# A graph-attention layer on one core: 128 dense groups instead of 120, counted by halves, with the counting moved ahead of the third and fourth tile's scores

## The chip, the core and the metric

The kernel runs on one core of a Trainium2 chip. The engines are named as in the profile: PE (matrix multiply; PEld is its weight load), DVE (vector), ACT (scalar), POOL (here the issuer of the indirect gathers) and SP (issuer of the other DMAs). The metric is the device time of one execution in microseconds, lower is better.

## The reference

The layer has 12,500 nodes of 64 features and 400,000 directed edges, each with 64 features of its own. The edges are sorted by destination, and destinations are drawn unevenly: the first nodes have hundreds of edges each, the last ones few.

```python
h_src = nfeats[src]; h_dst = nfeats[dst]
e = leaky_relu(concat([h_src, h_dst, efeats]) @ W_attn + b_attn, 0.01)[:, 0]
m = concat([h_src, efeats]) @ W_ne
ex = exp(e - segment_max(e, dst)[dst])
alpha = ex / segment_sum(ex, dst)[dst]
z = segment_sum(alpha[:, None] * m, dst)
out = relu(concat([nfeats, z]) @ W_out)
result = layernorm(nfeats + out)
```

What costs time is `nfeats[src]`, a gather of 400,000 rows, together with a softmax and a sum over each destination's edges.

## The kernel before

**Groups, parts, tiles.** The sorted edges are cut into 782 groups of 512 (128 partitions by T = 4). The first 120 groups (`DG`) are "dense": so few destinations fall in each that they are handled without a gather. The other 662 are "main" groups. These are worked in 43 parts: 39 of 16 groups, then 10, 10, 12 and 6 (`ENDS`). A part of 16 has four tiles of four groups, so 16 gathers for each tile and 64 for the part. One gather is one indirect DMA of 128 rows (L337), issued by POOL in program order. A part's gathers have the "places" 0 to 63.

**One part.** The loop over parts does, for tile i = 0 to 3: `scores` (L374 to L401; it multiplies edge features with a weight row, reduces them, adds the gathered source term at L390, and picks the destination's term by a one-hot row, L392 to L400), and between tiles work of other groups. Then comes one `softmax` of the part (L711 to L800; the maximum and the sum over destinations are scans over a row of 128 numbers, taken to a line and back by PE, L615 and L618). It is a generator: at four of its steps `drawn` calls `dense_step(n)`, n = 0 to 3, so that other work stands in the engines' queues between the softmax's own instructions. Then `weights` makes the one-hot times alpha (L808), and `products` (L820, L825) and `add_in` (L844) of each tile are laid into the next part's window and softmax. "Window" here means the stretch from the first L808 of a part to the next part's softmax; it is where the four tiles' scores are.

**What holds the gathers back.** POOL would run as far ahead as the buffers allow. `STEPS` and `PROBES` hold it: `step(place)` notes the matmul that stands last in PE's queue at that point, and the gather of that place then waits for it. The noted points are, with their places: the softmax's step 0 (8), the products in it (11, 14, 19, 24), the lookups (16, 21, 51), the counts (28, 33, 54), products (37 to 46) and the edge sums (48, or 57 with node products). A probe lets gather place+4 wait until PE has read what gather `place` brought (L328). Parts 1 and up are noted; the notes are cleared at part 1.

**Dense groups.** They go through four stages, several parts apart, in rounds of 12 (`ROUNDS`).
- *Look* (four groups a part, then three): `look_turn` on ACT makes a one-hot of the source's low seven bits, `look_products` (L460) multiplies it with the source terms of all blocks of 128 nodes, `look_scores` (L485 to L491) picks the block on DVE; `look_rows` (L470 to L479) adds the edge term. It gives each dense edge its score.
- *Joined*: a finished round's scores ride along in one part's softmax.
- *Count* (`dense_counts`): for each of the four t, ACT makes a one-hot over (block, node in group) in two passes (L499, L500), DVE a one-hot of the low bits times alpha (`lows`, L502), and PE multiplies the two (L507). The result, 98 columns for each node of the group, up to five nodes together and the sixth and seventh apart (L512 to L515), is added into `counts` by `dense_sum` (L525, L528).
- *Edges and nodes*: `edge_products`/`edge_sum` (L568, L577) sum the edge features. When a chunk of groups is counted, `node_products` (L584, 50 matmul instructions) multiplies `counts` with all node features, and `node_pick`, `node_turn`, `node_sum` (L592 to L609, with a clearing of `counts`, L597) take it to the accumulator.

**Order.** Nothing is reordered: each engine runs its instructions as the program writes them, and waits for operands and for buffers (four PSUM banks under the name `pg`, six `big` and six `lows` tiles).

## Time and profile before

| | |
|---|---|
| median of 3 runs | 4025.86 us (4024.07 to 4028.93) |
| the profiled execution | 4021.27 us, of which the span of instructions is 4019.5 us |
| granted PE clock, mean | 0.663 |
| PE / PEld / DVE busy | 60% / 50% / 53% |
| ACT / POOL busy | 32% / 62% |
| gathers L337 | 2584 on the page and 64 of part 0 before the table is made |

No engine is busy for more than 62% of the span. So the shares alone don't say what sets the time; it has to be read from who waits for whom within one part. A part's softmax begins with its ACT instruction L713, so the distance between two of them is the time of one part. In the rows, "128x490" is partitions by elements, "[2.78 <-PE lines L618]" is idle time before an instruction and what ended it, and "issue" means that nothing the profile shows was waited for.

### The profile page before, as it was taken

The numbers are of one execution on the slowest core, as the hardware profiler recorded it, in microseconds if no ns is written. First come the engines' busy times: TensorE is split into PE (matmuls) and PEld (weight loads), VectorE is DVE, ScalarE is ACT, GpSimd is POOL, SyncE is SP. The second block draws the span as 40 slices with busy tenths as digits, with TensorE's granted clock in tenths as the row PEclk, the third lists the DMA queues.
The fourth block names the chain that finished last, engine by engine and source line by source line (L and its number), as shares of the span: only waits on it lengthen the run. The fifth ranks groups of instructions, "written<-read, shape, count | busy, mean of one in ns | idle before, by whom it ended". The sixth has DMA issues, their size and how long they took to land. (4 is left out here: it accounts for less than half of the span.)

```text
span 4019.5 us, 39047 instructions
## 1 busy us (share of the span) xinstructions
PE 2404.4 (60%) x10302; PEld 1993.8 (50%) x10302; DVE 2133.3 (53%) x5517; ACT 1291.2 (32%) x2835; POOL 2511.9 (62%) x2676
## 2 busy tenths in 40 slices
PE   0144355665656676676777676656766657576544
PEld 0133345555555565554556554545655545465443
DVE  5343444555555555555655555645656464554345
ACT  1111122332333333333333433233443333333212
POOL 7466666666666666666666666666666666666452
PEclk9999996555555566665666666656666666666655
DMA  9222232332333233332332222322333232222121
GB/s 115 61 62 58 57 65 61 63 64 63 68 65 76 59 76 63 72 69 64 65 66 62 61 62 61 70 61 61 69 69 68 55 66 52 53 53 52 35 47 28
DMA packets 515063, 250.70 MB, mean 62 GB/s; under 512 B 351226, under 2 KB 472409, under 8 KB 514834
## 3 DMA queue, kind: packets, MB, share of 16 engines
q1 hardware_dynamic: 426588, 159.37, 17.1%
q0 software_dynamic: 84960, 88.33, 13.3%
q8 instruction: 87, 1.43, 0.1%
q14 instruction: 142, 1.16, 0.1%
q10 hardware_dynamic: 3286, 0.40, 0.1%
HBM read 241.09 MB, written 6.79 MB: 62 GB/s over the span
## 5 line engine op out<-in xcount | busy, mean ns | idle before, releaser
L337 POOL DMA_INDIRECT zx<-table,srcs x2584 | 2441.3, 945 | 1423.8 <-issue 778.1
L825 PE MATMUL pg<-w,zx 128*128 128x16 f32 (+9 forms) x5152 | 1107.0, 387 | 130.8 <-issue 87.7
L825 PEld LDWEIGHTS pg<-w,zx 128*128 128x128 f32 x5152 | 1091.0, 323 | 152.1 <-issue 93.1
L507 PE MATMUL pg<-big,lows 128*128 128x490 f32 (+3 forms) x960 | 546.8, 738 | 358.8 <-issue 107.5
L507 PEld LDWEIGHTS pg<-big,lows 128*128 128x128 f32 x960 | 267.1, 293 | 583.8 <-issue 499.1
L499 ACT ACTIVATE big<-places,place 128x490 f32<-128x490 int16 (+3 forms) x480 | 293.9, 612 | 96.9 <-PE pg L460 55.0
L487 DVE TENSOR_TENSOR pr<-pr,pg 128x392 f32<-128x392 f32 x120 | 67.5, 562 | 472.0 <-remote 172.5
L460 PE MATMUL pg<-s_src,big 128*128 128x98 f32 x960 | 266.6, 444 | 51.8 <-issue 51.5
L328 PE MATMUL pps<-zx,ident 1*1 1x1 f32 x236 | 21.3, 159 | 422.8 <-DMA zx<-table,srcs 368.4
L460 PEld LDWEIGHTS pg<-s_src,big 128*128 128x128 f32 x960 | 240.0, 328 | 49.0 <-issue 48.1
L500 ACT ACTIVATE big<-big 128x490 f32<-128x490 f32 (+3 forms) x480 | 257.1, 536 | 15.3
L385 DVE TENSOR_REDUCE fixed<-pr 128x16 f32<-128x1024 f32 (+3 forms) x172 | 204.2, 1187 | 102.1 <-ACT fixed L380 29.5
L615 PE MATMUL lines<-ident,bnd 128*1 128x128 f32 x172 | 51.8, 404 | 344.9 <-issue 249.5
L328 PEld LDWEIGHTS pps<-zx,ident 1*1 1x1 f32 x236 | 9.5, 76 | 447.9 <-DMA zx<-table,srcs 361.8
L844 DVE TENSOR_TENSOR acc<-acc,pg 128x16 f32 (+9 forms) x662 | 122.9, 186 | 174.1 <-remote 82.5
L390 DVE TENSOR_TENSOR fixed<-fixed,zx 128x16 f32<-128x16 f32 (+3 forms) x172 | 31.7, 184 | 329.6 <-DMA zx<-table,srcs 304.3
L383 DVE TENSOR_TENSOR pr<-ze,lines 128x1024 f32<-128x1024 f32 (+3 forms) x172 | 201.2, 1170 | 3.6 <-DMA ze<-in_edge_dram 3.5
L380 ACT ACTIVATE fixed<-wrow 128x96 f32<-128x96 f32 (+11 forms) x172 | 45.1, 262 | 477.7 <-issue 172.9
L615 PEld LDWEIGHTS lines<-ident,bnd 128*1 128x1 f32 x172 | 11.6, 93 | 352.8 <-issue 263.7
L502 DVE TENSOR_SCALAR lows<-fixed,low,kept 128x128 f32<-128x128 f32 x480 | 164.0, 401 | 34.5 <-PE pg L507 17.3
L381 ACT ACTIVATE zx<-ze 128x1024 f32<-128x1024 f32 (+3 forms) x172 | 176.5, 1026 | 6.2 <-issue 0.7
L713 ACT ACTIVATE soft<-turned 128x128 f32<-128x128 f32 x43 | 16.7, 388 | 482.2 <-DVE sdst L400 159.2
(305 smaller groups left out, 3035.3 us busy)
## 6 DMA issues: line engine op xcount, KB each, us to landing
ze<-in_edge_dram SPq DMA_DIRECT2D x157, 512.0 KB
zx<-table,srcs POOLq DMA_INDIRECT x2584
low_of<-low_rows SPq DMA_DIRECT2D x120, 128.0 KB
ep<-in_edge_dram SPq DMA_DIRECT2D x120, 128.0 KB
ed<-in_edge_dram SPq DMA_DIRECT2D x21, 512.0 KB
ed<-in_edge_dram SPq DMA_DIRECT2D x12, 384.0 KB
table<-xall SPq DMA_DIRECT2D x7, 455.0 KB
out_dram<-yo SPq DMA_DIRECT2D x24, 128.0 KB
```

Source lines behind the costliest of these rows:

```text
L337: issued.append(nc.gpsimd.indirect_dma_start(out=zx[0:r, g, t, 1:EW] if plain else zx[0:r, g, t, 0:EW], out_offset=None, in_=x[:, :] if pl ...
L381: nc.scalar.activation(zx[0:r, 0:n, :, EW:EW + D], ze[0:r, 0:n], AF.Copy)
L383: nc.vector.tensor_tensor(pr[0:r, 0:n], ze[0:r, 0:n], w_edge[0:r].unsqueeze(1).to_broadcast([r, n, T, D]), op=OP.mult)
L385: nc.vector.tensor_reduce(ysum[0:r, 0:n], pr[0:r, 0:n], axis=AX.X, op=OP.add)
L460: at_hand[0] = nc.tensor.matmul(found[:, t, :], hot[:, :, t], s_src, start=True, stop=True).ins
L487: nc.vector.tensor_tensor(hits, hits, found, op=OP.mult)
L499: nc.scalar.activation(hi, places[:, 0:wide], AF.Square, bias=place[:, t, g:g + 1])
L500: nc.scalar.activation(hi, hi, AF.Relu, scale=-1.0, bias=1.0)
L502: nc.vector.tensor_scalar(lows[t], count_, low[:, t, g:g + 1], kept[:, t, kept_at(g):kept_at(g) + 1], op0=OP.is_equal, op1=OP.mult)
L507: at_hand[0] = nc.tensor.matmul(to, lows[t], highs[t], start=(t == 0), stop=(t == T - 1)).ins
L825: at_hand[0] = nc.tensor.matmul(pg[:, g, :], zx[:, g, t, 1:EW + D], w[:, g, t, :], start=(t == 0), stop=(t == T - 1)).ins
L844: nc.vector.tensor_tensor(ag, ag, pg[:, g, :], op=OP.add)
```

## The change

1. **Sizes.** 128 dense groups instead of 120, in 16 rounds (twelve of 8, then 9, 9, 9, 5); main groups fall from 662 to 654, in 42 parts: 40 of 16 groups, then 8 and 6. Lookups are four a part up to group 96, then three. There are 18 chunks of node products instead of 12. A part's softmax carries a round on every second part.
2. **Counts by halves.** The 512 edges of a group are seen as two halves (t = 0, 1 and t = 2, 3), each with a first node of its own (`firsts`, `t0i`) and 2, 3 or 4 nodes wide (`HALVES`). Each half has a PSUM bank; `dense_sum` adds two results, at two places of `counts`. The sixth and seventh nodes' extra columns are gone.
3. **Order.** The edge sum, the node pick, the first lookup's scores and the node turn move from the softmax's step 0 to the stretch ahead of tile 2's scores; the second count's rows are made there too, the third's right after those scores, and only a fourth count stays in softmax step 3. `look_rows` moves from tile 2 to tile 1. One `dense_sum` stands ahead of tile 2's scores and one ahead of tile 3's.
4. **Holds.** The places 28, 33 and 54 (counts) no longer hold a gather; parts 0 and 1 leave no notes and no probes.
5. **Lookups in 16 bits.** The one-hot is bf16 and the source terms are three bf16 parts that add up in PSUM: twelve matmuls of 16-bit data for a lookup in place of four in fp32.
6. **Others.** The dense list is turned by PE transposes instead of loaded by ten DMAs; dense edges are loaded as (t p), in pieces of one row, not of four; a round that rides along goes through two more PE transposes; block 0's finish starts as soon as it can.

The core of the diff:

```diff
-ROUNDS = (12, 12, 12, 12, 12, 12, 12, 12, 12, 12)
+ROUNDS = (8,) * 12 + (9, 9, 9, 5)
-EACHS = ((84, 4), (120, 3))
+EACHS = ((96, 4), (128, 3))
-CHUNKS = ((36, 1), (12, 2), (8, 3), (6, 6))
+CHUNKS = ((36, 1), (12, 2), (8, 3), (4, 3), (6, 2), (3, 6), (2, 1))
+HALVES = ((40, 2), (84, 3), (128, 4))
+J = 2
-STEPS = {"ends": 8, "tile0": (11, 14, 19, 24), "look0": 16, "look1": 21, "count2": 28, "count3": 33,
-         "now": (37, 40, 43, 46), "edges": 48, "look": 51, "count": 54}
+STEPS = {"ends": 8, "tile0": (11, 14, 19, 24), "look0": 16, "look1": 21,
+         "now": (37, 40, 43, 46), "edges": 48, "look": 51}
-    ENDS = ((3, 3, 2, 2), (3, 3, 2, 2), (3, 3, 3, 3), (2, 2, 1, 1))
+    ENDS = ((2, 2, 2, 2), (2, 2, 1, 1))
...
-        hot = big()
+        hot = work.tile([P, P, T], BF16, name="turn", bufs=2)
...
         for t in range(T):
-            at_hand[0] = nc.tensor.matmul(found[:, t, :], hot[:, :, t], s_src, start=True, stop=True).ins
+            for i in range(3):
+                at_hand[0] = nc.tensor.matmul(found[:, t, :], hot[:, :, t], s_parts[:, i], start=(i == 0), stop=(i == 2)).ins
...
+        tos = [spare()[:, 0:wide] for _ in range(J)]
         for t in range(T):
-            at_hand[0] = nc.tensor.matmul(to, lows[t], highs[t], start=(t == 0), stop=(t == T - 1)).ins
+            at_hand[0] = nc.tensor.matmul(tos[t * J // T], lows[t], highs[t], start=(t * J % T == 0),
+                                          stop=(t * J % T == T - J)).ins
...
-                in_full[0] = G == BS
-                if k == 1 or G < BS:
+                in_full[0] = G == BS and k > 1
+                if k == 2 or G < BS:
                     marks.clear()
...
                 for i, (g0, n) in enumerate(lots[k]):
+                    if i == 2:
+                        if summed:
+                            edge_sum(*summed)
+                            summed = None
+                        picked_ = node_pick(*opened) if opened else None
+                        if seen:
+                            look_scores(*seen.pop(0))
+                        if len(batch_counts) > 1:
+                            open_counts.append(dense_counts(batch_counts[1]))
+                        if opened:
+                            node_z = node_turn(*picked_)
+                            opened = None
...
+                    if i > 1 and open_counts:
+                        dense_sum(*open_counts.pop(0))
...
                     hot = scores(g0, n, tiles[i], drel, b0, k == 0)
+                    if i == 2 and len(batch_counts) > 2:
+                        open_counts.append(dense_counts(batch_counts[2]))
...
-                    if n == 0 and opened:
-                        opened = node_pick(*opened)
-                    if n == 0 and summed:
-                        edge_sum(*summed)
-                        summed = None
                     if seen:
                         look_scores(*seen.pop(0))
-                    if n in (0, 3):
+                    if n == 0:
                         while open_counts:
                             dense_sum(*open_counts.pop(0))
...
-                    if n > 1:
-                        for g in batch_counts[-2:-1] if n == 2 and len(batch_counts) > 2 else batch_counts[1:][-1:] if n == 3 else ():
-                            open_counts.append(dense_counts(g))
-                            step(STEPS[f"count{n}"])
+                    if n == 3 and len(batch_counts) > 3:
+                        open_counts.append(dense_counts(batch_counts[3]))
```

What this does to the engines' queues shows at two places. The first is DVE in a part with node products and an edge sum. Before, the head of the softmax's step 0, right behind the scans L715 and L716 and ahead of the scans L723 and L724, reads (the last rows of an edge sum, `look_scores`, and the first of two counts' sums; the node pick stands ahead of them):

```order
L577 ISA
L577 TENSOR_TENSOR acce<-acce,pg 64x4
L485 TENSOR_TENSOR pr<-fixed,high 128x392
L487 TENSOR_TENSOR pr<-pr,pg 128x392
L489 TENSOR_REDUCE picked<-pr 128x4
L491 TENSOR_TENSOR y_dense<-y_dense,picked 128x4
L520 TENSOR_LOAD rel
L525 ISA
L525 TENSOR_TENSOR counts<-counts,pg 128x98x5
```

Of the changed kernel, the same work in another such part, now between tile 1's and tile 2's scores (`L503` to `L509` is `look_scores`, `L521` the second count's `lows`, `L613` the clearing of `counts`, `L538` the sum of a half):

```order
L587 TENSOR_TENSOR acce<-acce,pg 64x4
L602 TENSOR_TENSOR pr<-pg,own 128x256
L605 TENSOR_REDUCE sums__10318<-pr 128x64
L503 TENSOR_TENSOR pr<-fixed,high 128x392
L505 TENSOR_TENSOR pr<-pr,pg 128x392
L507 TENSOR_REDUCE picked<-pr 128x4
L509 TENSOR_TENSOR y_dense<-y_dense,picked 128x4
L521 TENSOR_SCALAR lows<-fixed,low,kept 128x128 x4
L613 MEMSET counts 128x3136
L533 TENSOR_LOAD rel
L538 ISA
L538 TENSOR_TENSOR counts<-counts,pg 128x98x3
```

Behind these rows the second half's sum follows, and then tile 2's scores. Edge sum, pick, lookup and one count's sum have left the softmax for the window, and the lows of a second count, which used to be made in the window or in softmax step 2, now stand ahead of tile 2's scores in all parts with two or more counts.

The second place is PE in such a part's window and the softmax behind it. Before, the edge products, a lookup and two counts are followed by the probe, and then by the softmax with the node turn and the next lookup:

```order
L568 MATMUL pg<-wd,ep 128x10 x8
L460 MATMUL pg<-s_src,big 128x98 x4
L507 MATMUL pg<-big,lows 128x490 x8
L328 MATMUL pps<-zx,ident 1x1 x2
L615 MATMUL lines<-ident,bnd 1x4x32 x2
L820 MATMUL pg<-zx,ident 1x4x8
L825 MATMUL pg<-w,zx 128x32 x16
L603 MATMUL pg<-node,sums__14404 64x32
L460 MATMUL pg<-s_src,big 128x98 x4
L618 MATMUL lines<-ident,line 128x1 x2
```

Of the changed kernel, from the end of the first lookup:

```order
L478 LDWEIGHTS turn
L478 MATMUL pg<-s_parts,turn 128x98
L526 MATMUL pg<-big,lows 128x294 x8
L611 MATMUL pps<-node,sums__15088 64x32
L526 MATMUL pg<-big,lows 128x294 x4
L345 MATMUL pps<-zx,ident 1x1 x2
L625 MATMUL lines<-ident,bnd 1x4x32 x2
L835 MATMUL pg<-zx,ident 1x4x8
L840 MATMUL pg<-w,zx 128x32 x16
```

The first two counts and the node turn (`L611`) come ahead of the third count's four matmuls, all of them ahead of the probe `L345`, and the counts are 294 columns wide here instead of 490. Softmax step 0 has no node turn any more. The lookup's four fp32 matmuls have become pairs of a 16-bit weight load and a matmul.

More of the change, by code (lines that the diff above doesn't have):

```diff
@@ L880, in sorted_path @@
     lists[1] = listed(1)
-    ids = pre.tile([DG, P, 2 * T], I32, name="ids", bufs=1)
-    nc.sync.dma_start(out=ids, in_=idx[0:DG])
+    ids = [pre.tile([min(P, DG - a), P, 2 * T], I32, name=f"ids{a}", bufs=1) for a in range(0, DG, P)]
+    for a, part in zip(range(0, DG, P), ids):
+        nc.sync.dma_start(out=part, in_=idx[a:min(a + P, DG)])
+    t0i = pre.tile([1, DG * J], I32, name="t0i", bufs=1)
+    nc.sync.dma_start(out=t0i, in_=dst.rearrange("(o n) -> o n", o=1)[:, 0:DG * GE:GE // J])
     nc.sync.dma_start(out=meet, in_=dst[DG * GE - 1:DG * GE + 1].unsqueeze(0))
@@ L1265, in sorted_path @@
                         nc.vector.memset(counts, 0.0)
[L1266 to L1272 removed]
+                    if i == 1:
+                        if batch_counts:
+                            open_counts.append(dense_counts(batch_counts[0]))
+                        if k and batch_looks:
+                            look_rows(batch_looks[0], len(batch_looks), loads)
                     if i == 3 and batch_counts:
```

230 lines of the change are left out of this document (123 added, 107 removed).

## The prediction

> **What bounds the kernel now.** I read the page first, for the shares.
>
> ```profile
> span 4019.5 us, 39047 instructions
> PE 2404.4 (60%) x10302; PEld 1993.8 (50%) x10302; DVE 2133.3 (53%) x5517; ACT 1291.2 (32%) x2835; POOL 2511.9 (62%) x2676
> L337 POOL DMA_INDIRECT zx<-table,srcs x2584 | 2441.3, 945 | 1423.8 <-issue 778.1
> ```
>
> No engine is full, so the bound lies inside a part. Cutting the span at the softmaxes (table of stretches, ACT busy in L713 alone) gives three pieces.
>
> ```profile
> 224.20:3706.80 3482.60, 14.42 (x38) 0.65 0.30 63
> 3706.80:4019.50 312.70, 1.90 (x5) 0.55 0.18 36
> ```
>
> Columns are stretch, length, ACT busy and count, clock, DMA share, GB/s. 224.2 us lie ahead; 38 softmaxes with 37 full parts between them take 3482.6, so 94.1 a part; the tail takes 312.7. Single stretches, whole (PE, PEld, DVE, ACT, POOL busy):
>
> ```profile
> 224.20:316.00 91.80, 39.81 (x191) 37.28 (x191) 37.92 (x100) 15.42 (x36) 60.45 (x65) 1.00 0.29 61
> 2004.80:2097.80 93.00, 64.04 (x235) 48.91 (x235) 55.88 (x138) 34.90 (x67) 61.34 (x66) 0.61 0.31 68
> 3041.20:3130.00 88.80, 57.38 (x239) 46.63 (x239) 55.35 (x132) 33.85 (x73) 58.17 (x62) 0.60 0.31 66
> 3130.00:3228.40 98.40, 68.64 (x301) 55.26 (x301) 54.07 (x132) 37.94 (x79) 62.57 (x67) 0.67 0.29 63
> ```
>
> The first has lookups and no counts, the second and third have counts, the fourth counts and node products. PE and DVE do half as much again in the second as in the first, for 1.2 us. What the first two share is 64 gathers. POOL's timeline:
>
> ```profile
> 2014.21 0.94 POOL L337 DMA_INDIRECT zx<-table,srcs  x1 [0.31 <-issue]
> 2017.93 0.94 POOL L337 DMA_INDIRECT zx<-table,srcs  x1 [2.78 <-PE lines L618]
> ```
>
> Unhindered, a gather takes 0.94 + 0.31 = 1.25 us, so 64 take 80; the other 13 or so are holds like the 2.78 (the gather of place 11 waits for the first products of softmax step 0). The last gather's landing ends the window. DVE's timeline, a plain part and then the node part:
>
> ```profile
> 2094.88 0.18 DVE L390 TENSOR_TENSOR fixed<-fixed,zx 128x16 f32<-128x16 f32 x1 [11.43 <-DMA zx<-table,srcs]
> 2097.48 0.32 DVE L711 STREAM_TRANSPOSE turned<-soft 128x128 f32<-128x128 f32 x1
> ```
> ```profile
> 3213.57 0.29 DVE L658 CUSTOM_DVE_ANT_0 step<-far 128x129 f32<-128x129 f32 x1 [13.00 <-ACT far L654]
> 3213.79 1.21 DVE L383 TENSOR_TENSOR pr<-ze,lines 128x1024 f32<-128x1024 f32 x1
> ...
> 3219.62 0.94 DVE L470 TENSOR_TENSOR pr<-ed,lines 128x768 f32<-128x768 f32 x1
> ...
> 3222.50 1.21 DVE L383 TENSOR_TENSOR pr<-ze,lines 128x1024 f32<-128x1024 f32 x1
> ...
> 3225.08 0.18 DVE L390 TENSOR_TENSOR fixed<-fixed,zx 128x16 f32<-128x16 f32 x1
> ```
>
> In the plain part DVE waits 11.43 us for the landing at tile 3: that is room in the window. In the node part it waits for nothing at L390; it lost 13.00 us earlier, to ACT, whose rows for the first count wait in line behind PE's node and edge products. **A plain part is bound by the gathers and their holds, a node part by its window.**
>
> **The change, part by part.** The sum is made on the profiled execution, 4021.3 us (span and 1.8 around it); the median is 4.6 above it.
>
> *Tail.* Now it has parts of 10, 10, 12 and 6 groups after the last full one:
>
> ```profile
> 3706.80:3799.10 92.30, 54.78 (x252) 44.97 (x252) 38.59 (x107) 29.39 (x70) 51.24 (x55) 0.65 0.20 38
> 3799.10:3885.50 86.40, 40.12 (x178) 35.66 (x178) 33.36 (x96) 13.25 (x34) 43.30 (x46) 0.50 0.19 37
> 3885.50:3947.20 61.70, 24.41 (x115) 22.24 (x115) 32.83 (x84) 13.76 (x36) 37.67 (x40) 0.50 0.28 61
> 3947.20:3982.90 35.70, 20.10 (x171) 17.39 (x171) 24.83 (x73) 8.18 (x26) 7.56 (x9) 0.55 0.06 8
> 3982.90:4019.50 36.60, 17.39 (x227) 14.95 (x227) 17.96 (x73) 6.03 (x16) 0.00 (x0) 0.50 0.06 12
> ```
>
> With 8 and 6 there are three stretches: softmax of the last full part to that of the 8, between 80 and 92.3, I take 85; from there to the last, between 35.7 and 61.7, I take 50; the end 36.6. That is 172 for 312.7: **−141** (−155 to −122). In exchange there is a 38th full stretch, counted below. (32 gathers fewer are 40 us at 1.25; the rest is the saving of two short parts, which hardly overlap.)
>
> *Start.*
>
> ```profile
> 161.24 0.94 POOL L337 DMA_INDIRECT zx<-table,srcs  x1 [0.30 <-issue]
> 202.69 2.87 POOL L337 DMA_INDIRECT zx<-table,srcs  x1 [40.50 <-PE pps L328]
> ...
> 220.83 0.95 POOL L337 DMA_INDIRECT zx<-table,srcs  x1 [0.30 <-issue]
> ```
>
> POOL waits 40.50 us for a probe of part 1, which parts 0 and 1 no longer have. The rest of part 1's gathers and part 2's first (220.83) can come up to 40 us earlier, but part 1's scores still have to be done and buffers freed: 0 to −27, I take a third of the wait, **−13**.
>
> *Plain parts, the softmax.* DVE at step 0:
>
> ```profile
> 2099.12 0.43 DVE L716 TENSOR_TENSOR_SCAN soft<-step,soft 128x128 f32<-128x128 f32 x1
> 2099.65 0.15 DVE L577 TENSOR_TENSOR acce<-acce,pg 64x5 f32 x1
> ...
> 2101.49 0.57 DVE L485 TENSOR_TENSOR pr<-fixed,high 128x392 f32<-128x392 f32 x1
> ...
> 2103.81 1.44 DVE L525 TENSOR_TENSOR counts<-counts,pg 128x490 f32 x2 [0.36 <-issue]
> 2105.16 0.33 DVE L723 TENSOR_TENSOR_SCAN tops<-rw,tops,lines 1x64 f32<-1x64 f32 x1
> ```
>
> Between L716's end (2099.55) and L723 (2105.16) lie 5.6 us: edge sum 1.8, lookup 2.3, two counts 1.5. One count's two halves stay, about 1.3. So the softmax gets some 4 us shorter at its head, and the hold of 2.78 at place 11 hangs on just this step: up to 2.5 of it goes. The work arrives in the window instead, with the sums of two counts and the lows of one more, 8 us against the 11.43 of room. It costs nothing there while that cover holds; without it, up to 8 a part. I take 91 for a plain part (93.0 less 2; between 88.8 and 91.8 stand the rows).
>
> *Node parts.* Groups of instructions over the whole run (busy us, mean ns):
>
> ```profile
> L507 PE MATMUL pg<-big,lows 128*128 128x490 f32 (+3 forms) x960 | 546.8, 738 | 358.8 <-issue 107.5 <-DVE lows L502 102.8 <-DVE acc L844 101.6
> L502 DVE TENSOR_SCALAR lows<-fixed,low,kept 128x128 f32<-128x128 f32 x480 | 164.0, 401 | 34.5 <-PE pg L507 17.3 <-issue 17.0
> L525 DVE TENSOR_TENSOR counts<-counts,pg 128x490 f32 (+3 forms) x120 | 69.3, 578 | 143.8 <-remote 45.7 <-issue 39.6 <-PE pg L507 38.7
> L597 DVE MEMSET counts<- 128x3136 f32 x11 | 29.4, 2672 | 6.6 <-issue 6.6
> ```
>
> Behind the 13-us wait DVE now gets: edge sum 1.8, lookup 2.3, pick 0.8 (two instructions, taken like lows), lows of two counts 8 × 0.40 = 3.2, clearing 2.7, four half sums at no more than 0.58, about 2: 13 us. `look_rows` (3219.62 to 3222.50) goes ahead of it, −2.9. So the window grows by 10, with tiles 2 and 3, the softmax and all behind it queued after the waits for the node and count matmuls. The softmax loses 4 and with them pick and clearing, 4 more: −8. PE does less inside the 13-us wait: 546.8 us for 120 counts are 4.6 each, at 294 or 392 columns for up to 490 some 3 to 3.7; two counts give −2 to −3, the third is added behind. Net about −1 on rows between 95 and 98.4: I take 96.5, between 94 and 101. No row shows the new order; below nothing is possible since the node pick leaves the softmax.
>
> Of 18 chunks 17 fall into full parts (11 before, of 12). The sum over 38 stretches: 17 × 96.5 + 21 × 91 = 3552 for 3482.6, **+69**.
>
> *Lookups.* Four fp32 matmuls become twelve 16-bit ones; no row shows their time. Bounded by half and one and a half of today's; both ends a microsecond a lookup, on PE, mostly beside the softmax's waits: I take 0 and keep 20 us in the range. *Edge loads in smaller pieces:* DMA share is 0.31 or less and loads stand a part ahead: 0. *Riding rounds:* two transposes and two short DVE instructions in 16 parts: under 1 each, 0 to +10.
>
> *Clock.* PE gets sparser. The products alone, in a sparse and in a denser part:
>
> ```profile
> 224.20:316.00 91.80, 27.97 (x128) 27.94 (x128) 1.00 0.29 61
> 2004.80:2097.80 93.00, 28.15 (x128) 27.72 (x128) 0.61 0.31 68
> ```
>
> 128 product matmuls take 27.97 us at a granted clock of 1.00 and 28.15 at 0.61: the clock changes nothing here, so it has no term. The Trainium skill ("TensorE: Matmul & The Clock Gate", Part 1: The HAM clock gate) says that PE's array falls to half its clock after an idle window of about 3.4 us; the trace differs twice, since the sparser part is the one at 1.00, and the time doesn't follow the clock.
>
> **Sum:** −141 − 13 + 69 = −85; 4021.3 − 85 + 4.6 = **3941**. About 0.2%, 8 us, is what a measurement tells from no change.
>
> **Rivals.**
> - *The window has room everywhere* (0.20). Node parts lose their 13-us wait since the counts are narrower, and all parts go at the first stretch's 91.5: 38 × 91.5 = 3477, −6; with −154 that is −160, **3866**. For it: a node part and its neighbour average 93.6 already. Against: 0.00 wait at L390 in node parts.
> - *The window of node parts becomes the bound at full price* (0.11, slower). DVE waits ahead of tile 2's scores for node products and counts; the 10 us are added and the softmax, which waits for PE, gives nothing back: 17 × 108.4 + 21 × 91 = 3754, +271 − 154 = +117, **4143**. It decides from 101.5 a node part on: 17 × 101.5 + 21 × 91 = 3636 uses up the 154.
> - *Fewer holds starve PE* (0.06). When POOL runs long without a hold, PE's instructions come late:
>
> ```profile
> 3716.93 1.08 PE L825 MATMUL pg<-w,zx 128*128 128x44 f32 x4
> 3720.01 0.23 PE L825 MATMUL pg<-w,zx 128*128 128x44 f32 x1 [2.00 <-issue]
> ...
> 3724.91 0.23 PE L825 MATMUL pg<-w,zx 128*128 128x44 f32 x1 [2.56 <-issue]
> ```
>
>   Places 28 and 33 hold nothing any more. Between 24 and 37 lie 13 gathers, 16 us; one such step of 2.56 in each of 34 parts gives back 87: **4028**, no change. Against: the first stretch has no count holds either, and takes 91.80.
> - *The half clock comes all the same* (0.02): products at 0.5 for 0.61 cost 28.15 × 0.22 = 6.2 a part, 236 in 38: **4177**. This is the rule of the Trainium skill just named.
> - The forecast keeps 0.61.
>
> **Range and chances.** The forecast's own ends are node parts at 94 and 99, plain at 90 and 92.5, with the ends of start and tail: 3850 to 4045 if all fall together, 3875 to 4010 as they likely do. To hold eight in ten it goes down over the first rival's middle and up to 4020; out stay the two slow rivals and halves of the others. Faster by over 0.2%: 0.80; within: 0.05 (half of the third rival and the forecast's edge); slower: 0.15.
>
> **What would show it.** Right: no 40-us wait of POOL by 202; three stretches in the tail of about 172; plain parts at 91 with DVE still waiting for a landing at tile 3's L407; L728 to L735 under 2 us where L716 to L723 is 5.6. Wrong: node parts over 101 with DVE waiting for PE ahead of tile 2's scores; a hold of POOL that moves to place 24 or 37 and leaves plain parts at 93; single matmuls 2 us apart.

## The result and the profile after

The changed kernel takes 4261.31 us (4245.85 to 4276.96, 4 runs), the kernel before 4027.39 (4024.07 to 4039.26, 4 runs): ratio **1.0575, 95% interval 1.053 to 1.0621**. It is slower by 234 us, where 3941 was forecast.

The runs were made in sets, each with the kernel before beside it, and the chip was met in two conditions: in some sets the kernel before takes 3978 to 4028 us (this result is one), in others 3383 to 3386; they are called the 4000 sets and the 3385 sets, a ratio is always to the kernel before in the same set, and "points" are hundredths of that ratio.

The profiled run of the changed kernel took 4264.77 us. Its page, shares and the costliest lines (busy, mean ns of one, idle just before and what ended most of it):

```profile
span 4263.1 us, 40302 instructions
PE 2349.8 (55%) x10847; PEld 1974.9 (46%) x10847; DVE 2223.2 (52%) x5738; ACT 1187.4 (28%) x2711; POOL 2483.9 (58%) x2641
L354 POOL DMA_INDIRECT zx<-table,srcs x2552 | 2414.1, 946 | 1700.6 <-issue 1002.6
L526 PE MATMUL pg<-big,lows 128*128 128x294 f32 (+2 forms) x1024 | 495.4, 657 | 492.9 <-DVE lows L521 300.1
L505 DVE TENSOR_TENSOR pr<-pr,pg 128x392 f32<-128x392 f32 x128 | 72.0, 563 | 673.4 <-remote 414.0
```

PE, ACT and POOL are busy for less than before and DVE for 90 us more (2223.2 for 2133.3); the rest of the 244 us between the two profiled spans is waiting. POOL's idle time ahead of gathers rose from 1423.8 to 1700.6 us, with 32 gathers fewer. The span cut at the softmaxes (ACT in L725 alone):

```profile
235.40:4119.80 3884.40, 14.73 (x38) 0.61 0.28 59
4119.80:4263.10 143.30, 1.17 (x3) 0.55 0.12 27
```

Against before: the start is 235.4 for 224.2, +11.2; 38 full stretches take 3884.4 (102.2 each) for 37 of 94.1, +401.8; the tail takes 143.3 for 312.7, −169.4. Together +243.6, the difference of the spans. The 17 stretches with node products sum to 1834.7, 107.9 each; the other 21 to 2049.7, 97.6 each. A plain and a node stretch (PE, PEld, DVE, ACT, POOL busy):

```profile
1992.54:2088.77 96.23, 58.58 (x267) 49.74 (x267) 56.65 (x153) 35.11 (x80) 61.88 (x66) 0.54 0.32 67
2088.77:2193.78 105.01, 64.65 (x300) 54.26 (x300) 57.63 (x144) 30.31 (x70) 59.21 (x64) 0.63 0.27 59
```

DVE in the window of that node stretch, from tile 1's scores to tile 3's (start, length, idle before):

```profile
2153.87 1.23 DVE L402 TENSOR_REDUCE fixed<-pr 128x16 f32<-128x1024 f32 x1 [7.99 <-ACT fixed L397]
...
2170.14 0.15 DVE L587 TENSOR_TENSOR acce<-acce,pg 64x5 f32 x1 [4.45 <-PE pg L478]
...
2171.95 0.42 DVE L602 TENSOR_TENSOR pr<-pg,own 128x256 f32<-128x256 f32 x1
...
2174.91 1.36 DVE L521 TENSOR_SCALAR lows<-fixed,low,kept 128x128 f32<-128x128 f32 x4
2176.87 2.67 DVE L613 MEMSET counts<- 128x3136 f32 x1 [0.60 <-issue]
2179.58 1.02 DVE L538 TENSOR_TENSOR counts<-counts,pg 128x294 f32 x2
2180.52 1.22 DVE L400 TENSOR_TENSOR pr<-ze,lines 128x1024 f32<-128x1024 f32 x1
...
2190.43 0.18 DVE L407 TENSOR_TENSOR fixed<-fixed,zx 128x16 f32<-128x16 f32 x1
```

The head of the softmax that follows, the two scans and the first of the next row of scans:

```profile
2195.07 0.43 DVE L728 TENSOR_TENSOR_SCAN soft<-step,soft 128x128 f32<-128x128 f32 x1
2196.17 1.04 DVE L538 TENSOR_TENSOR counts<-counts,pg 128x294 f32 x2 [0.67 <-issue]
2197.11 0.33 DVE L735 TENSOR_TENSOR_SCAN tops<-rw,tops,lines 1x64 f32<-1x64 f32 x1
```

In the window the moved work stands between 2170.14 and 2180.52, 10.4 us, behind two waits for ACT and PE, and nothing waits for a landing at L407. PE and POOL, at the part's end:

```profile
2186.12 4.26 PE L526 MATMUL pg<-big,lows 128*128 128x294 f32 x8 [8.21 <-DVE lows L521]
2190.31 0.23 PE L345 MATMUL pps<-zx,ident 1*1 1x1 f32 x4
2191.24 0.95 POOL L354 DMA_INDIRECT zx<-table,srcs  x1 [13.21 <-issue]
```

PE waits for the lows that DVE makes behind all that (300.1 us over the run, in the row of L526 above; in the kernel before L507 waits 102.8); the probe (L345) stands behind those counts in PE's queue; POOL starts the next part's gathers 0.70 us after the probe's end. The profile puts this wait down to "issue"; that it is the probe's follows from the program, in which place 0 waits for the probe of place 60. A hold of 13 us has appeared at the *first* place of the next part. In the kernel before, at the end of the node part of 3130 to 3228 us, the probe also stands behind counts, but these are done by 3215.5: the probe waits only for its gather to land, and place 0 isn't held:

```profile
3208.36 6.25 PE L507 MATMUL pg<-big,lows 128*128 128x490 f32 x8
3214.44 1.03 PE L515 MATMUL pps<-big,lows 128*128 128x98 f32 x8
3217.78 0.18 PE L328 MATMUL pps<-zx,ident 1*1 1x1 f32 x2 [2.31 <-DMA zx<-table,srcs]
3220.27 0.95 POOL L337 DMA_INDIRECT zx<-table,srcs  x1 [0.30 <-issue]
```

In stretch 3252.65 to 3365.06 of the changed kernel, a plain one with three counts, a probe in the same spot holds place 52:

```profile
3340.40 4.56 PE L526 MATMUL pg<-big,lows 128*128 128x392 f32 x8 [2.58 <-DVE lows L521]
3344.89 0.23 PE L345 MATMUL pps<-zx,ident 1*1 1x1 f32 x4
3345.35 0.94 POOL L354 DMA_INDIRECT zx<-table,srcs  x1 [21.03 <-PE pps L345]
```

The table is worked out from the traces: means over full parts from the third softmax on, split at the first `weights` instruction behind each softmax; "holds" is POOL's idle time ahead of gathers beyond the 0.305 us that always lies there. Since a part is 64 gathers of 1.25 us, 80 us, and its holds, the last column says how much is lost, not why. Kernels from sets of 3978 to 4028 us stand side by side in it; that spread of 1.2% is about 1 us a part.

| kernel (set) | node parts: softmax + window, holds | plain parts: softmax + window, holds |
|---|---|---|
| before (4000) | 44.2 + 51.8 = 96.0, 16.0 | 42.7 + 50.7 = 93.4, 13.5 |
| after (4000) | 38.3 + 69.6 = 107.9, 27.0 | 41.2 + 57.5 = 98.7, 18.1 |
| before (3385) | 34.5 + 46.0 = 80.5, 0.4 | 33.1 + 46.9 = 80.1, 0.2 |
| after (3385) | 26.2 + 55.5 = 81.8, 2.2 | 28.1 + 54.0 = 82.1, 1.8 |
| without probes (4000) | 35.4 + 67.4 = 102.8, 20.4 | 42.7 + 55.7 = 98.3, 19.3 |
| work back, three probes (4000) | 39.7 + 62.8 = 102.5, 23.1 | 42.8 + 55.3 = 98.0, 17.2 |
| work back, no probes (4000) | 34.5 + 62.6 = 97.1, 16.8 | 39.7 + 55.3 = 95.0, 14.9 |

Split by place, the holds show where the loss lies. Over these parts, 36 before and 37 after, they sum to 512 and 822 us in the 4000 sets. The places that wait for a probe (0, 52 and 61 here) make up 45 us of it before and 336 after; the edge sums' place 57 rose from 2.6 to 5.4 us a node part. In a node part place 0 alone went from 0.8 to 12.1 us, nearly the whole growth of 96.0 to 107.9.

### The profile page after: what moved, and what is told of

Same layout as the page of the kernel before. It is cut to its first block, busy times and chain, and to the rows that moved or that the text cites. A ratio compares the mean times of both kernels' runs of the same rounds, so it can differ in the third digit from the quotient of the medians.

```text
span 4263.1 us, 40302 instructions
## 1 busy us (share of the span) xinstructions
PE 2349.8 (55%) x10847; PEld 1974.9 (46%) x10847; DVE 2223.2 (52%) x5738; ACT 1187.4 (28%) x2711; POOL 2483.9 (58%) x2641
## 4 chain that ended last, share of the span: by engine, by line
DVE 26%; PE 21%; issue 20%; another core or an unknown queue 15%; POOL 9%; ACT 2%; DMA 2%; DVEq 2%; POOLq 0%; SPq 0%; ACTq 0%
PE pg L840 10%; POOL zx L354 9%; PE pg L594 4%; DMA zx<-table,srcs 2%; DVE pr L400 2%; DVE fixed L402 2%; DVE pr L414 2%; DVE hot L409 2%; DVE sdst L417 1%; PE pg L526 1%; DVE lows L521 1%; DVE acc L859 1%; DVE counts L538 1%; DVE picked L507 1%
## 5 line engine op out<-in xcount | busy, mean ns | idle before, releaser
L354 POOL DMA_INDIRECT zx<-table,srcs x2552 | 2414.1, 946 | 1700.6 <-issue 1002.6
L526 PE MATMUL pg<-big,lows 128*128 128x294 f32 (+2 forms) x1024 | 495.4, 657 | 492.9 <-DVE lows L521 300.1
L526 PEld LDWEIGHTS pg<-big,lows 128*128 128x128 f32 x1024 | 299.3, 310 | 650.3 <-issue 536.7
L402 DVE TENSOR_REDUCE fixed<-pr 128x16 f32<-128x1024 f32 (+1 forms) x168 | 201.4, 1199 | 200.3 <-ACT fixed L397 81.5
L518 ACT ACTIVATE big<-places,place 128x294 f32<-128x294 int16 (+2 forms) x512 | 269.9, 527 | 110.3 <-PE pg L526 88.0
L594 PE MATMUL pg<-xall,counts 128*128 128x256 f32 x900 | 249.0, 438 | 53.9 <-issue 53.8
L594 PEld LDWEIGHTS pg<-xall,counts 128*128 128x128 f32 x900 | 198.0, 225 | 102.4 <-issue 70.7
L519 ACT ACTIVATE big<-big 128x294 f32<-128x294 f32 (+2 forms) x512 | 230.8, 451 | 19.8 <-remote 2.1
L478 PE MATMUL pg<-s_parts,turn 128*128 128x98 bf16 x1536 | 169.9, 276 | 111.0 <-issue 101.3
L478 PEld LDWEIGHTS <-turn 128*128 128x128 bf16 x1536 | 146.1, 149 | 133.1 <-issue 130.9
L400 DVE TENSOR_TENSOR pr<-ze,lines 128x1024 f32<-128x1024 f32 (+1 forms) x168 | 198.5, 1182 | 0.1
L398 ACT ACTIVATE zx<-ze 128x1024 f32<-128x1024 f32 (+1 forms) x168 | 174.6, 1039 | 7.0 <-issue 1.0
L521 DVE TENSOR_SCALAR lows<-fixed,low,kept 128x128 f32<-128x128 f32 x512 | 173.9, 401 | 0.0
L538 DVE TENSOR_TENSOR counts<-counts,pg 128x294 f32 (+2 forms) x256 | 122.4, 478 | 60.8 <-remote 28.4
L345 PE MATMUL pps<-zx,ident 1*1 1x1 f32 x224 | 17.3, 159 | 232.8 <-DMA zx<-table,srcs 176.8
```

The source lines that it names most:

```text
L354: issued.append(nc.gpsimd.indirect_dma_start(out=zx[0:r, g, t, 1:EW] if plain else zx[0:r, g, t, 0:EW], out_offset=None, in_=x[:, :] if pl ...
L398: nc.scalar.activation(zx[0:r, 0:n, :, EW:EW + D], ze[0:r, 0:n], AF.Copy)
L400: nc.vector.tensor_tensor(pr[0:r, 0:n], ze[0:r, 0:n], w_edge[0:r].unsqueeze(1).to_broadcast([r, n, T, D]), op=OP.mult)
L402: nc.vector.tensor_reduce(ysum[0:r, 0:n], pr[0:r, 0:n], axis=AX.X, op=OP.add)
L478: at_hand[0] = nc.tensor.matmul(found[:, t, :], hot[:, :, t], s_parts[:, i], start=(i == 0), stop=(i == 2)).ins
L518: nc.scalar.activation(hi, places[:, 0:wide], AF.Square, bias=place[:, t, g:g + 1])
```

## The experiments

Theories: **window** (the work that moved ahead of tile 2's scores lengthens the window), **probes** (the probes, now queued behind counts that wait for DVE, hold POOL), **sizes** (rounds of eight, 18 chunks), **halves and lookups** (more and smaller instructions on PE). In the expectations on record W stands for the window, P for the probes, S and I for PE getting its instructions late, C for a loss that depends on the chip's condition. Each experiment is told by its edit against the changed kernel unless it says otherwise.

| run | before | this | ratio, 95% interval |
|---|---|---|---|
| after_again | 3384.58 | 3437.55 | 1.0155 [1.0132, 1.0177] |
| no_probes | 3385.53 | 3365.72 | 0.9943 [0.9926, 0.996] |
| no_probes_2 | 3978.33 | 4158.68 | 1.0454 [1.0429, 1.0478] |
| three_probes | 3978.33 | 4188.58 | 1.0517 [1.0491, 1.0544] |
| work_back | 3385.53 | 3409.64 | 1.0067 [1.005, 1.0084] |
| work_back_2 | 3383.64 | 3402.01 | 1.0052 [1.0032, 1.0072] |
| work_and_probes | 3385.18 | 3376.54 | 0.9977 [0.9968, 0.9987] |
| work_and_probes_2 | 4028.03 | 4151.2 | 1.0315 [1.0254, 1.0375] |
| work_and_no_probes | 3981.04 | 4006.16 | 1.0072 [1.0043, 1.01] |
| counts_back | 3385.53 | 3447.4 | 1.018 [1.0163, 1.0197] |
| counts_back_2 | 3383.64 | 3446.55 | 1.0186 [1.0166, 1.0206] |
| more_holds | 3978.33 | 4220.88 | 1.0603 [1.0577, 1.0629] |
| old_order_new_sizes | 3385.53 | 3435.95 | 1.0152 [1.0135, 1.0169] |
| new_order_old_sizes | 3978.33 | 4226.31 | 1.062 [1.0602, 1.0638] |
| fp32_looks | 3383.64 | 3509.17 | 1.0364 [1.0344, 1.0385] |
| before_16bit_looks | 3383.64 | 3382.81 | 0.9996 [0.9985, 1.0006] |
| before_16bit_looks_2 | 3385.18 | 3381.87 | 0.9989 [0.9979, 0.9999] |

**The probes.** No gather waits for a probe:

```diff
-gather(g0, n, srcs, b0, k == 0, () if G < BS or k < 2 else PROBES[-2:] if chunk_was else ...)
+gather(g0, n, srcs, b0, k == 0, ())
```

> Changed kernel, but no gather waits for a probe any more (PE doesn't read what the gathers of places 48 to 63 brought). Theory P (the probes stand behind the third count on PE, which waits for DVE's lows, and so hold POOL at place 0 after node parts, 11 to 15 us in 16 parts, and at place 52 in three plain parts, 15 to 21 us): these some 260 us of holds go, and most of it shows, about 4060 us. Theory W (the window of node parts is full of DVE work, and that alone sets the time): the node parts stay at 107, only the three plain parts gain, about 4215 us. Theory S (POOL running without holds starves PE and DVE of instructions): not faster, 4260 us or more.

POOL's gathers of the changed kernel and of the one without probes, in 3385 sets:

```profile
L354 POOL DMA_INDIRECT zx<-table,srcs x2552 | 2408.6, 944 | 874.0 <-issue 741.8
```
```profile
L354 POOL DMA_INDIRECT zx<-table,srcs x2552 | 2409.8, 944 | 803.5 <-issue 695.3
```

Holds all but vanish and parts fall to 80 us (80.9 and 79.4). In that condition the probes are worth 2.1 points, more than the whole loss. The same edit in a 4000 set, beside a smaller one (parts with three counts keep only the last probes, as those with groups of more than five nodes did before the change: `PROBES[3:] if len(batch_counts) > 2`):

> The changed kernel without probes once more, for the case that this set is given a chip on which the kernel before takes 4027 us. There theory P (probes behind the counts hold POOL) gives about 4060 us, theory S (instructions come late while POOL runs without holds, and the change has taken holds away) 4200 us or more. Where the kernel before takes 3385 us it repeats 3366 us.

> Changed kernel, with one figure changed: parts with three counts leave only the probes of places 57, 60 and 63, as parts with four counts do (before the change every part with a group of more than five nodes did so). Theory P: the holds at place 52 of three parts go (9.6, 3.9 and 12.0 us where the kernel before takes 3385 us; 21, 15 and 21 us where it takes 4027), those at place 0 stay: 3437 - 25 = 3412 us, or 4261 - 55 = 4206 us. Theory W: the three parts have room of 15 to 18 us at tile 3, so their time follows the gathers as well; no difference between the theories in those three, none elsewhere. Rival: the hold moves to place 61 with the same length, no gain.

Here the probes alone give back 1.2 points, less than was expected of them (4060 us). Without probes POOL is held elsewhere: at place 8, which waits for softmax step 0 (8.2 us on average in 31 parts, 15.4 at most), and at place 37 (6.0 us on average, for 3.8). Holds moved; node parts got 5.1 us shorter, plain ones hardly. The smaller edit came out 0.6 points lower, but its interval (up to 1.0544) and that of the changed kernel (from 1.053) overlap, and the trace shows no gain in holds: places 52 and 61 together hold POOL 134 us in the changed kernel and 137 in this one, nearly all of it now at 61. That was the rival in its expectation.

**The moved work.** Edge sum, node pick, turn and sum and the first lookup's scores go back to softmax steps 0 and 1 of full parts (the edit in short):

```diff
 if i == 2:
-    if summed:
+    if summed and G < BS:
         edge_sum(*summed)
-    picked_ = node_pick(*opened) if opened else None
+    picked_ = node_pick(*opened) if opened and G < BS else None
...
 def dense_step(n):
+    if n == 0 and opened: opened = node_pick(*opened)
+    if n == 0 and summed: edge_sum(*summed)
+    if n == 0 and opened: node_z = node_turn(*opened)
+    if n == 1 and node_z: node_sum(*node_z)
```

> Changed kernel, with edge sum, node pick, node turn, node sum and the first lookup's scores back in the softmax's steps 0 and 1 for all full parts; the counts stay where the change has put them. Theory W: DVE's window loses 7 to 8 us in the 17 node parts and about 4 in plain ones that have no room left, the softmax gets back half of it: 4261 - 120 = about 4140 us. Theory P: the third count and with it the probe come some 7 us earlier in node parts, no more: about 4190 us. Theory S: no change, 4260 us.

This kernel clears `counts` too late and so leaves part of the counts out. The second keeps the clearing ahead of tile 2's scores:

> Changed kernel, with edge sum, node pick, turn and sum and the first lookup's scores back in softmax steps 0 and 1 of full parts; the clearing of the counts stays ahead of tile 2's scores. Theory W: on the slower chip 2 points or more come back, 1.035 times the kernel before; on the faster one nearly 1 point (its near twin, which cleared too late, had 1.0067). Theory I: half a point at most on the slower chip.

Both give back about 1 point of the 1.55, in a 3385 set. Holds at place 52 stay (11.7, 5.8 and 10.2 us in the three parts with three counts).

**Both together**, first with the smaller probe edit, in both conditions:

> Changed kernel, with edge sum, node pick, turn and sum and the first lookup's scores back in softmax steps 0 and 1 (as in work_back_2), and only three probes in parts with three counts (as in three_probes). On the faster chip: the holds at place 52 that work_back_2 has left are 28 us, 3402 - 28 = 3374 us, a little below the kernel before at 3384. On the slower chip: theory W gives 1.035 times the kernel before or less, theory I (late instructions in the lookups' pairs) 1.05.

> work_and_probes once more, for the slower chip: theory W gives 1.035 times the kernel before or less there, theory I (late instructions, which the moved work has little part in) 1.045 or more. On the faster chip 0.998 again.

In the 3385 set the two edits together take the loss away and leave 0.9977, as leaving out the probes did alone (0.9943). In the 4000 set they take 2.6 points and leave 3.2; POOL is still held 8 to 12 us at place 0 after node parts. (The work back with all probes was not run in a 4000 set.) So the last run has the work back and no probes at all:

> The work back at softmax steps 0 and 1 (as in work_back_2), and no probes at all. Two theories of what is left beside the moved work and the early probes. (a) Holds theory: what costs is POOL standing behind something that PE or DVE finishes late, wherever it is put. On a chip where the kernel before takes about 3385 us, probes were worth 2.1 points and the moved work 1.0, and the holds they cause overlap, so together 3355 to 3370 us (0.991 to 0.996), with POOL's holds under 0.5 us a part and parts of 80 us. On a chip where the kernel before takes about 4000 us, the holds only move (to the gathers that wait for softmax steps 0 and 3), and the work put back there makes them longer: no better than the 1.0315 of work_and_probes_2, 1.03 to 1.045. (b) Length theory: what costs is the total length of the chain from one softmax to the next, and holds are only its symptom; then taking both away on the slower chip gives less than either alone suggests but more than the better of them: 1.015 to 1.03, and node parts come to 98 us or less.

It came out at 1.0072, below what either theory gave. The cut at the softmaxes and POOL's line:

```profile
217.92:3856.96 3639.04, 14.79 (x38) 0.63 0.31 63
3856.96:4004.10 147.14, 1.17 (x3) 0.56 0.14 28
...
L354 POOL DMA_INDIRECT zx<-table,srcs x2552 | 2408.9, 944 | 1443.9 <-issue 782.8
```

Full parts take 95.8 us, node parts 97.1 ("98 us or less" was the mark of the length theory) and POOL's idle time is back at 1443.9, the level of before. **The work back and no probes together give back 5.0 of the 5.75 points.** Not all of that need be what the change cost: the kernel before has probes too, they hold its gathers for 45 us over its full parts, about 1.1 points, and it was not run without them. The two edits are worth more together than apart: going on from the smaller probe edit to no probes gives 0.6 with the work in the window (1.0517 to 1.0454) and 2.4 with it back (1.0315 to 1.0072). What remains, 0.7, was not divided further in this condition.

**The same two kernels again**, with a profile of each in the same set:

> The changed kernel without any edit, on the chip that this set of runs is given. In the runs of the edits just shown the kernel before took 3385 us, not 4027: the gathers took the same 0.944 us each, but PE, DVE and ACT lost less time between their instructions, and POOL ran nearly without holds. Theory C (the loss belongs to a chip on which engines wait long for their next instruction while POOL gathers; without that wait a part is bound by its 64 gathers, 80 us, in both orders): where the kernel before takes about 3385 us, the changed one is within 1.5% of it, 3360 to 3440 us; where it takes about 4027 us, it is 5 to 6% slower, about 4260 us. Rival (the order alone makes the loss): 5 to 6% slower on either, 3560 us or more.

> The kernel before without any edit, for its profile on the same chip as the other runs of this set. Theory C: where it takes about 3385 us, its softmaxes stand 80 us apart, POOL has hardly a hold, and the softmax up to the first weights takes 10 us or more less than the 38 to 48 us of the first profile, at the same instruction durations; where it takes 4027 us, the profile is like the first. Rival (instructions themselves are faster there): the mean durations differ.

The loss is 1.55 points there. DVE in a node part's window, the same two waits:

```profile
1765.98 1.23 DVE L402 TENSOR_REDUCE fixed<-pr 128x16 f32<-128x1024 f32 x1 [5.38 <-ACT fixed L397]
1780.21 0.15 DVE L587 TENSOR_TENSOR acce<-acce,pg 64x5 f32 x1 [2.42 <-PE pg L478]
```

5.38 and 2.42 us where the 4000 set had 7.99 and 4.45: the same waits in the same order, at another price.

**Counts.** The second count goes back behind tile 2's scores, the last but one to softmax step 2 (the edit in short):

```diff
-if len(batch_counts) > 1: open_counts.append(dense_counts(batch_counts[1]))     # ahead of tile 2's scores
-if i == 2 and len(batch_counts) > 2: open_counts.append(dense_counts(batch_counts[2]))
+if i == 2 and len(batch_counts) > 3: open_counts.append(dense_counts(batch_counts[1]))
+for g in batch_counts[-2:-1] if n == 2 ... else batch_counts[1:][-1:] if n == 3 ...   # softmax steps 2, 3
```

> Changed kernel, with the second count behind tile 2's scores (where there are four) or in softmax step 3, and the third (the last but one) in softmax step 2, as before; edge sum, pick and lookup stay in the window. Theory P: the probes no longer stand behind the third count's wait, the holds at places 0 and 52 go: about 4060 us. Theory W: the window loses 4 us of lows and sums in each part, the softmax gets them: 4200 us. Theory S: no change.

> Changed kernel with the second and third count where they were before (second behind tile 2's scores or in softmax step 3, last but one in softmax step 2), once more for the slower chip. Where it is the faster one, 1.018 as measured. On the slower one theory W gives a gain of a point or more, to 1.045 or less, as the window is relieved; theory I none, since the same instructions only stand elsewhere.

No gain, in two 3385 sets: the holds at place 52 go, those at places 0 and 61 grow (from 38 to 58 us and from 9 to 28 in the first). So there the counts' place alone is not what costs; in a 4000 set it was not run. Nor are the removed holds what costs; places 28 and 33 put back at softmax steps 2 and 3, in a 4000 set:

```diff
+if n > 1: step({2: 28, 3: 33}[n])
```

> Changed kernel, with two holds put back: place 28 waits for the matmul that stands last on PE at softmax step 2, place 33 for that of step 3. Where the kernel before takes 3385 us POOL runs behind these points and nothing changes: 3437 us within 0.3%. Where it takes 4027 us, theory S gives a gain, 40 us or more, as PE and DVE get their instructions between places 24 and 37; theories P and W give none or a loss of up to 40 us.

1.0603 against 1.0575 of the changed kernel: no help.

**Sizes.** The old order with the new sizes (the kernel before with `ROUNDS`, `EACHS`, `CHUNKS`, `NODS` of the changed one), and the new order with the old sizes:

```diff
-ROUNDS = (8,) * 12 + (9, 9, 9, 5)
+ROUNDS = (12, 12, 12, 12, 12, 12, 12, 12, 12, 12)
```

> The kernel before, with the sizes of the change alone: 128 dense groups in rounds of 8 and 9, lookups and chunks as in the change, last parts of 10, 10, 6 and 4 groups instead of 10, 10, 12 and 6. Order, holds, counts five nodes wide and fp32 lookups as before. If the order made the loss (P and W): 32 gathers fewer are -40 us, six more node parts about +20, so about 4005 us. Rival: more node parts and rounds make it whatever the order: 4150 us or more.

> The changed kernel with the sizes of before: 120 dense groups in ten rounds of 12, lookups, chunks and last parts as before; order, holds, halves and 16-bit lookups as in the change. Where the kernel before takes 3385 us: if the order with its probes is what costs (P, W), 11 node parts in place of 17 and 37 full stretches leave about two thirds of the holds, and 32 gathers come back: 3385 + 35 = 3420 us; if the sizes cost, about 3385 us. Where it takes 4027 us: P and W give 4027 + 100 = 4130 us, sizes alone 4027 us.

The first was a miss: in a 3385 set the new sizes alone cost 1.5 points in the old order, as much as the whole change costs there, and again by probes: place 0 is held for up to 9.8 us, places 0 and 61 together for 41 of the 50 us lost. What they cost in the old order in a 4000 set was not run. The second shows that in a 4000 set the order, the halves and the lookups cost the whole loss without the sizes, more than the 4130 us expected; the intervals of 1.062 and 1.0575 overlap, so a gain by sizes in the new order is not shown.

**Lookups.** Fp32 in the changed kernel (with one `lows` buffer fewer for space), and 16 bits in the kernel before (with one `big` buffer fewer):

```diff
-for i in range(3):
-    at_hand[0] = nc.tensor.matmul(found[:, t, :], hot[:, :, t], s_parts[:, i], start=(i == 0), stop=(i == 2)).ins
+at_hand[0] = nc.tensor.matmul(found[:, t, :], hot[:, :, t], s_src, start=True, stop=True).ins
```

> Changed kernel with the lookups as before: a one-hot in fp32 and four fp32 matmuls for a lookup instead of twelve 16-bit pairs (one buffer of lows fewer, for space). Theory I (where PE gets its instructions late, twelve pairs cost more than four matmuls that do the same): on the slower chip a gain of 2 points or more, to 1.035 times the kernel before; on the faster chip, where no gaps are, within half a point of 1.0155. Theory W (the order is what costs): no gain on either, 1.0575 and 1.0155.

> The kernel before with 16-bit lookups alone, twelve pairs (one big buffer fewer, for space, since lookups no longer take one). Theory I: slower by 2 points or more on the slower chip, 1.02 times the kernel before; theory W: within half a point of 1.0. On the faster chip within half a point of 1.0 in both.

> The kernel before with 16-bit lookups alone, for the slower chip: theory I 1.02 times the kernel before or more, theory W within half a point of 1.0. On the faster chip 1.0 again.

16-bit lookups in the kernel before make 0.9996 and 0.9989, nothing or 0.1 points, in the 3385 sets. The fp32 form is 2.1 points worse than the changed kernel, where no difference was expected, but the missing buffer is in that figure, so it says nothing on lookups alone. In a 4000 set neither was run, so there the lookups stay a rival for what remains.

## Why the prediction was wrong

- *Tail*: right in direction, mis-sized: −169 for −141, since three stretches take 68.2, 38.0 and 37.0 and not 85, 50 and 36.6.
- *Start*: the 40.50-us wait is gone, as predicted, but −13 became +11.2. The stall moved: part 2's gathers wait 19.65 us at place 0 and 17.85 at place 51. The prediction misread its holder: the 40.50 us stood at place 51 too, which in the program waits for a lookup; the profile names the probe that stands right behind that lookup in PE's queue. The sign depends on the cut: the next stretch, 235.36 to 310.68, takes 75.3 us for 91.8 before, so that the changed kernel is 5.3 us ahead at the third softmax. With the work back and no probes the first full stretch starts at 217.92, −6.3.

```profile
195.70 0.94 POOL L354 DMA_INDIRECT zx<-table,srcs  x1 [19.65 <-issue]
290.53 0.94 POOL L354 DMA_INDIRECT zx<-table,srcs  x1 [17.85 <-PE pps L345]
```

- *Softmax*: the head is shorter as worked out (L728's end to L735 is 1.6 us), and a node part's softmax loses 5.9 us of the 8 that were predicted (8.3 in a 3385 set). A plain part's loses 1.5 of 4.
- *Plain parts, 91*: **failed**. "It costs nothing there while that cover holds": the cover was counted as fixed. DVE's wait for the landing at tile 3 shrank from 10.0 to 7.4 us on average (5.5 without the three parts that a probe holds at place 52) and wasn't used up, yet the part grew to 98.7, because the gathers themselves came later: holds went from 13.5 to 18.1, of which places 52 and 61, which wait for probes, went from 1.4 to 6.5. There was no term for a hold that grows, only for one that goes (2.5 at place 11, which did shrink, from 3.37 to 1.67). Of the places named as a sign of a moved hold, 24 and 37, the first is about unchanged and the second went from 2.1 to 3.9.
- *Node parts, 96.5*: **the step that failed most**, 107.9. The window was to grow by 10 us. In a 3385 set it does: +9.5, and the softmax −8.3, both terms nearly as worked out. In the 4000 sets it grew by 17.8. The step "Behind the 13-us wait DVE now gets" put the moved work where DVE had been idle, and followed DVE and PE to the end of the window. It did not follow PE's queue one entry further, to the probe, and from there to POOL. The order rows quoted with the change show the probe behind the counts. The premise, a node part bound by its window, was read from one part: of the 11 node parts before, DVE waits for nothing at L390 in three, and in the others 1 to 11 us. After the change that wait is gone in all 17, so the first rival's room was not there either.
- *The second rival* named the size (108.4 for a node part) and the mark, DVE waiting for PE ahead of tile 2's scores (4.45 us at L587). Its price was 10 us of growth on a part of 98.4 with nothing given back; measured was a growth of 17.8 with 5.9 given back. So its size of a node part is right by luck, by a mechanism that is only partly its own: the probes are the rest. Its total, 4143, is still 118 short, mostly since it left the plain parts at 91. It had a chance of 0.11, although the 0.00 wait at L390, read there against the first rival, speaks for it as well.
- *The third rival*, PE starved: instructions do come late more often, see below, but their sum doesn't follow the loss: without probes it is 217 us at 1.0454, with the work back as well 282 at 1.0072. So they are not the cause by themselves.
- *Clock*: no term was needed; 0.627 for 0.663 while the gather and product durations stay (387 ns each for products).

The profile could have told: the 13 us or so of holds above a part's 80 us of gathers were read and quoted, but only as something that could go. Each moved piece should have been asked which hold it delays.

## What to carry to other kernels

Where an engine issues at a fixed rate and is held back by notes in another engine's queue, price a move by what each held instruction will stand behind, not by the room beside the moved work: here 10 us of moved DVE work cost 12 a part, because a probe stood last in PE's queue behind matmuls that waited for that work. Take the probe's or the note's place along when the work in front of it moves, and look again at holds that were harmless. Two edits that each give back a little can give back nearly all together, so try them together before looking for a third cause.

## What the runs showed of the hardware

The same kernel took 4027 us in one set and 3385 in another, with nearly the same durations of instructions. Products in the kernel before, first in the 4000 set (x5152, mean ns, idle before), then in a 3385 set; and the gathers of the latter:

```profile
L825 PE MATMUL pg<-w,zx 128*128 128x16 f32 (+9 forms) x5152 | 1107.0, 387 | 130.8 <-issue 87.7
```
```profile
L825 PE MATMUL pg<-w,zx 128*128 128x16 f32 (+9 forms) x5152 | 1070.5, 380 | 15.7 <-DVE w L808 15.6
L337 POOL DMA_INDIRECT zx<-table,srcs x2584 | 2441.5, 945 | 796.6 <-issue 683.5
```

A gather takes 945 ns in both; what differs is idle time between instructions that wait for nothing shown. The same rows of the waits of PE for the kernel before, for the changed one and for the one with work back and no probes, all in 4000 sets (us in total, times, longest):

```profile
PE pg L825 <- issue: 87.7, 62, 3.6
```
```profile
PE pg L840 <- issue: 178.8, 149, 3.3
```
```profile
PE pg L840 <- issue: 168.3, 101, 8.8
```

Single matmuls in the 4000 sets stand up to a few us apart, as here in the changed kernel:

```profile
2109.92 0.35 PE L478 MATMUL pg<-s_parts,turn 128*128 128x98 bf16 x2
2111.70 0.48 PE L478 MATMUL pg<-s_parts,turn 128*128 128x98 bf16 x4 [1.43 <-issue]
2113.83 0.40 PE L478 MATMUL pg<-s_parts,turn 128*128 128x98 bf16 x3 [1.65 <-issue]
```

Gaps of 0.2 to 3 us between two matmuls of one line, with nothing shown that was waited for, sum to 183 us over the kernel before in its 4000 set and to none in a 3385 set; after the change to 346 and none. The last run has 282 and is within 0.7% of before all the same. They do not come only while POOL runs unheld, as the prediction's third rival had it: about half of that time, 99 of the 183 us and 168 of the 346, lies where POOL is held (idle for over 0.8 us ahead of a gather). What makes them, and whether the condition belongs to a chip or to its state, stays open; chip 13 was met in both (3385.5 and 4028.0 us). In the 3385 sets POOL has almost no holds and the gathers of a part alone take 80 us, so this change can gain there in start and tail alone. Tails of before and after in one such set:

```profile
3153.45:3383.90 230.45, 1.92 (x5) 0.59 0.24 49
```
```profile
3295.01:3434.10 139.09, 1.18 (x3) 0.56 0.15 30
```

That is −91.4 for one more part of 80: some 11 us to be had. The best version, without probes, takes 3365.72 us (0.9943), 20 less than before. None that was run beats the kernel before in a 4000 set; the nearest is 1.0072.
